# Turned tokens kept dense by feature block instead of interleaved, in an attention block on one core

## The chip, the cores and the metric

One core of a Trainium2 chip runs the whole program. The metric is the device time of one execution in microseconds (us); the time before is the median of three runs.

## The reference

The block gets 4 sequences of 1024 tokens with 512 features, f32. Cut to what matters:

```python
xn = layernorm(x)                                            # (4, 1024, 512)
q  = rope(rmsnorm(xn @ Wq + bq, qn_w))                       # 16 heads of 128
lk = rope(rmsnorm(xn @ Wlk + blk, kn_w)); lv = xn @ Wlv + blv
w  = softmax((xn @ Wcmp + bcmp).reshape(C, 4))               # C = 256 groups of 4 tokens
entries = einsum('cr,crh->ch', w, xn.reshape(C, 4, 512))     # weighted sum of each group
ck = rope(rmsnorm(entries @ Wk + bk, kn_w)); cv = entries @ Wv + bv
# per token and head: softmax over the 8 best of its causal ck scores, and a
# softmax over the band of this and the 128 tokens before
merged = (sparse @ cv + local @ lv) * 0.5
out = x + merged @ Wo + bo + fp8_rounded(xn) @ fp8_rounded(input2)
```

## The kernel before

**Chunks and units.** The 4096 tokens are cut into 32 chunks of 128 (t = 0 to 31, c = t mod 8 is the place within a sequence). For each chunk the heads go in eight units of two heads (u = 0 to 7). One loop runs over all 256 units s = 8t + u, and each of its passes works on several units at once, in an order written out by hand: TensorE does the scores of unit s (`scores`, L718 to L728), the queries and keys of s + 3 (`queries`, L576), the output product of s - 2 (`to_output`, L921), the values of s + 1 (`values_of`, L682) and the contexts of s - 1 (`values`, L888). VectorE masks the scores and finds the eight best (`weigh`, L750 to L773), settles the sparse weights, normalizes and rotates queries and keys, and turns 32 x 32 blocks.

**What goes through DRAM.** A full 128 x 128 turn is done in two halves: VectorE transposes 32 x 32 blocks within their partitions, and a write to DRAM followed by a read in another order moves the blocks to the right partitions. This is done for the probabilities (`turn`, L829 and L837, tile pr; `fetch`, L871, tile probT), for queries and keys (`turn_keys`, L657 and L660, tile thb, and L665, tile qk; `fetch_keys`, L675) and for the normalized tokens. All these transfers are issued by SyncE (SP), in program order. In a pass its queue holds, in this order: the write of the probabilities pr, whatever chunk preparation issues, the four key writes, the four fetches of probT, the two key fetches, and, in u = 2, the four fetches of the tokens of the next chunk. A transfer that has to wait holds up those behind it.

**Chunk preparation.** `chunk_prep(t)` is a generator that advances by two steps in each pass (`steps`). It loads a chunk, normalizes it (tile x_norm), weighs it for the pooled entries (L372 to L384), and in its step A3, which falls into u = 2, transposes the blocks (L392, x_norm to xb) and writes xb to DRAM (L397). In u = 3 it multiplies by the group weights (L403) and sums groups of four tokens (L411, tile few), and writes few (L420). Four chunks ahead of use is the rule; in the first chunks two are prepared in one chunk. Chunk 0 is turned by TensorE instead (`turn_tokens_here`, L460 and L462), and its entries are made by `add_tokens_here` (L437, L443). `chunk_entries` fetches the pooled sums back (L501) and multiplies them by the key and value weights (L511).

**The turned tokens.** `fetch_tokens` (L471) brings the tokens of a chunk into xnT: feature in the partition, and in each partition the element of token s and feature block k at s * 4 + k. So a 128 x 128 block for TensorE, which loads it as the stationary operand, is read at a step of four f32:

```python
xnT[:, :, k] if k or not t else xone,      # queries, L578
xnT[:, :, k],                              # values_of, L684
```

`put_ones` (L478) copies block 0 into a dense tile xone, for the chunks after the first, and sets its first row to one, which brings in the bias. `chunk_eight` rounds xnT to the values of an eight-bit float and multiplies the result x8 (bf16) by input2 (L558).

Of the kernel before, what the change touches and what calls it, by code (L numbers as in the profile page):

```python
# [12 lines left out]
F32 = mybir.dt.float32  # L13
# [6 lines left out]
P = 128  # L20
D = 128
RATIO = 4
ROPE = 64
HALF = ROPE // 2
BLK = 32
NB = P // BLK
# [12 lines left out]
def kernel(  # L39
# [299 lines left out]
    def chunk_prep(t):  # L339

        xt = x_tiles.pop(("norm", t))
        st = work.tile([P, 8], F32, tag="lnst", name=f"lnst_{t}")
        nc.vector.bn_stats(st[:, 0:6], xt)
        nc.vector.bn_aggr(st[:, 6:8], st[:, 0:6])
        r = rstd_of(st[:, 7:8], 1, 1.0, EPS_LN, f"lnr_{t}")
        yield "A0"
        yield "B0"
        if t:

            off = work.tile([P, 2], F32, tag="off", name=f"off_{t}")  # L350
            nc.gpsimd.tensor_scalar(off[:, 0:1], st[:, 6:7], -1.0, None, ALU.mult)
            nc.scalar.activation(
                xt, xt, AF.Identity, bias=off[:, 0:1], scale=1.0, accum_out=off[:, 1:2]
            )
            nc.gpsimd.tensor_scalar(off[:, 1:2], off[:, 1:2], 1.0 / HID, None, ALU.mult)
            mean = off[:, 1:2]
        else:
            mean = st[:, 6:7]
        yield "A1"
        nc.vector.tensor_scalar(xt, xt, mean, r, ALU.subtract, ALU.mult)  # L360
        yield "B1"
        if not t:
            turn_tokens_here(xt)
            yield "T"

        xb = scratch(f"xb_{t}")
        log = work.tile([P, 1], F32, tag="log", name=f"log_{t}", bufs=1)
        row = work.tile([P, 2, BLK], F32, tag="row", name=f"row_{t}", bufs=1)  # L370
        red = work.tile([P, BLK // RATIO], F32, tag="red", name=f"red_{t}", bufs=1)
        nc.vector.scalar_tensor_tensor(  # L372
            xb, xt, 1.0, wcmp_sb, ALU.mult, ALU.mult, accum_out=log
        )
        nc.vector.tensor_scalar(row[:, 0, :], ones, log, bcmp_sb, ALU.mult, ALU.add)
        nc.vector.transpose(row[:, 1, :], row[:, 0, :])
        fours = row[:, 1, :].rearrange("p (n r) -> p n r", r=RATIO)

        def wide(v):
            return v.unsqueeze(2).to_broadcast([P, BLK // RATIO, RATIO])  # L380

        nc.vector.tensor_reduce(red, fours, AX.X, ALU.max)
        nc.vector.tensor_tensor(fours, fours, wide(red), ALU.subtract)
        nc.scalar.activation(row[:, 1, :], row[:, 1, :], AF.Exp)  # L384
        yield "A2"
        yield "B2"
        if not t:
            yield from add_tokens_here(row, red, xb, wide)
            return


        nc.vector.transpose(  # L392
            xb.rearrange("p (b j k) -> p b k j", b=NB, k=KK),
            xt.rearrange("p (k b i) -> p b k i", b=NB, k=KK),
        )
        tokens[t] = dram.tile([P, HID], F32, tag="xb", name=f"xb_dram_{t}", bufs=GC + 2)
        nc.sync.dma_start(tokens[t], xb)  # L397
        yield "A3"
        nc.vector.tensor_reduce(red, fours, AX.X, ALU.add)
        nc.vector.reciprocal(red, red)  # L400
        nc.vector.tensor_tensor(fours, fours, wide(red), ALU.mult)
        yield "B3"
        nc.vector.tensor_tensor(  # L403
            xt.rearrange("p (b j k) -> p b j k", b=NB, k=KK),
            xb.rearrange("p (b j k) -> p b j k", b=NB, k=KK),
            row[:, 1:2, :].unsqueeze(3).to_broadcast([P, NB, BLK, KK]),
            ALU.mult,
        )
        yield "A4"
        few = work.tile([P, P], F32, tag="few", name=f"few_{t}", bufs=1)  # L410
        nc.vector.tensor_reduce(  # L411
            few.rearrange("p (n k) -> p n k", k=KK),
            xt.rearrange("p (n r k) -> p n k r", r=RATIO, k=KK),
            AX.X,
            ALU.add,
        )
        g, i = divmod(t, GC)
        if g not in pooled:
            pooled[g] = dram.tile([GC, P, P], F32, tag="pooled", name=f"pooled_{g}")
        nc.sync.dma_start(pooled[g][i], few)  # L420
        yield "B4"

    def add_tokens_here(row, red, xb, wide):

        few = scratch("few_here")
        nc.gpsimd.memset(few, 0.0)
        fours = row[:, 1, :].rearrange("p (n r) -> p n r", r=RATIO)
        nc.vector.tensor_reduce(red, fours, AX.X, ALU.add)
        nc.vector.reciprocal(red, red)
        nc.vector.tensor_tensor(fours, fours, wide(red), ALU.mult)  # L430
        nc.vector.transpose(row[:, 0, :], row[:, 1, :])
        wp = pp("weights_here")
        nc.tensor.matmul(
            wp[:, 0:P], row[:, 0, 0:1].to_broadcast([P, P]), ident, start=True, stop=True
        )
        yield "W"
        nc.vector.tensor_tensor(  # L437
            xb.rearrange("p (s k) -> p s k", k=KK),
            chunks[0][0],
            wp[:, 0:P].unsqueeze(2).to_broadcast([P, P, KK]),  # L440
            ALU.mult,
        )
        nc.vector.tensor_reduce(  # L443
            few[:, 0 : NE * KK].rearrange("p (n k) -> p n k", k=KK),
            xb.rearrange("p (n r k) -> p n k r", r=RATIO, k=KK),
            AX.X,
            ALU.add,
        )
        few_here.append(few)
        few_here.append(dram.tile([P, P], F32, tag="few_here", name="few_dram", bufs=1))  # L450
        nc.sync.dma_start(few_here[1], few[:, 0 : NE * KK])
        yield "B4"
# [3 lines left out]
    def turn_tokens_here(xt):  # L456

        xp = pp("xp")
        for k in range(KK):
            nc.tensor.transpose(xp[:, ts(k, P)], xt[:, ts(k, P)], ident)  # L460
        xnT = work.tile([P, P, KK], F32, tag="xnT", name="xnT_0")
        nc.scalar.copy(  # L462
            xnT.rearrange("p s k -> p k s"), xp.rearrange("p (k s) -> p k s", k=KK)
        )
        chunks[0] = (xnT, None)

    def fetch_tokens(t):
        xnT = work.tile([P, P, KK], F32, tag="xnT", name=f"xnT_{t}")
        turned = tokens.pop(t).rearrange("(a i) (b x) -> b i a x", a=NB, b=NB)
        for b in range(NB):  # L470
            nc.sync.dma_start(  # L471
                xnT[ds(b * BLK, BLK)].rearrange("i (a j) k -> i a (j k)", a=NB), turned[b]
            )
        chunks[t] = (xnT, work.tile([P, P], F32, tag="xone", name=f"xone_{t}"))

    def put_ones(t):
        xnT, xone = chunks[t]
        nc.scalar.copy(xone, xnT[:, :, 0])  # L478
        nc.gpsimd.memset(xone[0:1], 1.0)

    def chunk_entries(g, n):
# [64 lines left out]
    def chunk_eight(t):  # L546

        yield
        xt, xnT = x_tiles["sum", t], chunks[t][0]
        x8 = work.tile([P, KK * P], BF16, tag="x8", name=f"x8_{t}", bufs=1)  # L550
        src = xnT.rearrange("p s k -> p (s k)")
        yield from quantize(x8, src, scales[:, 0:1], f"x_{t}")
        nc.gpsimd.tensor_tensor(xt, xt, bo_sb, ALU.add)
        yield
        x8 = x8.rearrange("p (s k) -> p s k", k=KK)
        fp = pp(f"fp_{t}")
        for k in range(KK):
            nc.tensor.matmul(  # L558
                fp, x8[:, :, k], w2_sb[:, k, :], start=(k == 0), stop=(k == KK - 1)
            )  # L560
        yield
        nc.vector.scalar_tensor_tensor(xt, fp, inv, xt, ALU.mult, ALU.add)
# [8 lines left out]
    def queries(n):  # L571
        t, u = place(n)
        xnT, xone = chunks[t]
        qp = psum.tile([P, 512], F32, tag="qp", name=f"qp_{n}")
        for k in range(KK):
            nc.tensor.matmul(  # L576
                qp,
                xnT[:, :, k] if k or not t else xone,  # L578
                wqk_sb[u][:, k, :],
                start=(k == 0),  # L580
                stop=(t > 0 and k == KK - 1),
            )
        if not t:
            nc.tensor.matmul(  # L584
                qp, sel[:, u : u + 1].to_broadcast([P, P]), bias_b, start=False, stop=True
            )
        ss = work.tile([P, 4], F32, tag="ss", name=f"ss_{n}")
        units[n] = {"qp": qp, "ss": ss}
# [88 lines left out]
    def values_of(n):  # L677
# [3 lines left out]
        for k in range(KK):  # L681
            nc.tensor.matmul(  # L682
                vp[:, 0:256],
                xnT[:, :, k],  # L684
                wlv_sb[u][:, k, :],
                start=(k == 0),
                stop=(k == KK - 1),
            )
# [419 lines left out]
```

## Time and profile before

| | |
|---|---|
| median of three runs | 2717.2 us (2714.86 to 2717.34) |
| the profiled execution | 2725.88 us |
| its span, first to last instruction | 2723.7 us |
| granted TensorE clock | 0.992 |
| DMA engines, mean busy share | 56% on SyncE's queue |
| transfers of the tokens to DRAM, xb_dram | 31 of 256 KB, 2.2 us from issue to landing |
| fetches of the tokens, xnT | 124 of 64 KB, 2.3 us |

The busy shares of the engines are shares of the span. PE is the matmuls of TensorE and PEld its loads of the stationary operand, which run beside matmuls. Each f32 matmul shows as two records. The chain is followed back from the last instruction, at each step to what released it or to the instruction before it on its engine. In the groups, a line has the program line, the engine, the operation, the tile written and those read, the shape and the count; then busy us, mean ns of one; then the idle time of the engine just before them and who ended it. SPq is SyncE's queue of transfers; its length of a transfer is the time that the issue took.

### The profile page before, as it was taken

To read this page: it belongs to the slowest core of one execution; us is meant where nothing else is said; L and a number is where in the kernel's file an instruction comes from. 1 tells how busy PE (TensorE), PEld (TensorE's weight loads), DVE (VectorE), ACT (ScalarE), POOL (GpSimd) and SP (SyncE) were. 2 spreads that over 40 slices of the span, in tenths; PEclk is the share of its full clock that TensorE was granted. 3 is DMA by queue.
4 is the path that set the end of the run, shared out by engine and by line. 5 is a ranking of instruction groups with operands and counts; after the bars stand their busy time and mean duration, and the time that the engine had idled before them with its cause. 6 is when DMAs were issued, how large, how long until landed. Compare 5 with 4: busy or idle time off the path is not lost.

```text
span 2723.7 us, 46686 instructions
## 1 busy us (share of the span) xinstructions
PE 2652.3 (97%) x11802; PEld 2086.2 (77%) x11837; DVE 2318.3 (85%) x8884; ACT 1257.7 (46%) x5067; POOL 799.1 (29%) x1151
## 2 busy tenths in 40 slices
PE   8999999999999999999999999999999999999997
PEld 5777777777777777777777778777777777777776
DVE  7888888898888888888988888888988888888885
ACT  3444444444444444444444444444444444444443
POOL 4522332223332223232233322232323323222221
PEclk9999999999999999999999999999999999999998
DMA  8455455665545555566555555655665555566653
GB/s 257 120 142 150 132 149 167 171 165 153 154 135 158 151 157 149 161 166 169 160 145 139 155 151 154 170 159 157 168 164 146 150 141 147 151 161 165 162 153 107
DMA packets 667067, 422.85 MB, mean 155 GB/s; under 512 B 326528, under 2 KB 616112, under 8 KB 666800
## 3 DMA queue, kind: packets, MB, share of 16 engines
q1 hardware_dynamic: 666192, 419.46, 56.0%
q8 instruction: 97, 1.59, 0.3%
q14 instruction: 170, 1.39, 0.2%
q10 hardware_dynamic: 608, 0.41, 0.1%
HBM read 225.42 MB, written 194.25 MB: 154 GB/s over the span
## 4 chain that ended last, share of the span: by engine, by line
PE 76%; DVE 11%; DMA 5%; SPq 3%; ACT 3%; issue 2%; POOL 1%; DVEq 0%; ACTq 0%
PE qp L576 25%; PE vp L682 13%; PE cp L888 12%; PE op L921 12%; PE sc L728 5%; PE sc L725 4%; PE sc L718 3%; DMA probT<-pr 2%; SPq L665 1%; SPq L871 1%; ACT prob L775 1%; DVE probB L829 1%; DVE sc L750 1%; DVE taken L773 1%; PE fp L558 1%
## 5 line engine op out<-in xcount | busy, mean ns | idle before, releaser
L576 PE MATMUL qp<-wqk,xnT 128*128 128x512 f32 x1552 | 711.5, 595 | 3.5 <-DMA wqk<-in_L_attn_Wlk_dram 3.5
L576 PEld LDWEIGHTS qp<-wqk,xnT 128*128 128x128 f32 x1552 | 478.0, 309 | 221.4 <-issue 64.9
L775 ACT ACTIVATE prob<-sc,neg 128x256 f32<-128x256 f32 (+1 forms) x512 | 235.9, 461 | 879.2 <-DVE taken L773 861.1
L682 PEld LDWEIGHTS vp<-wlv,xnT 128*128 128x128 f32 x2048 | 517.8, 325 | 91.9 <-issue 56.2
L682 PE MATMUL vp<-wlv,xnT 128*128 128x256 f32 x2048 | 516.4, 395 | 0.1
L921 PE MATMUL op<-wo,cT 128*128 128x512 f32 x1024 | 481.6, 593 | 3.4 <-ACT cT L903 3.3
L325 POOL TENSOR_TENSOR rb<-th,cs 128x256 f32<-128x256 f32 x256 | 204.1, 797 | 949.7 <-DVE th L604 941.6
L750 DVE CUSTOM_DVE_ANT_0 sc<-sc,mask_b 128x256 f32<-128x256 f32 (+1 forms) x512 | 210.9, 412 | 180.8 <-PE sc L728 170.8
L811 ACT ACTIVATE prob<-prob,tot 128x256 f32<-128x256 f32 (+1 forms) x512 | 225.6, 488 | 300.3 <-DVE tot L801 297.6
L921 PEld LDWEIGHTS op<-wo,cT 128*128 128x128 f32 x1024 | 193.6, 190 | 206.8 <-issue 144.9
L888 PE MATMUL cp<-probT,lv 128*128 128x128 f32 x1920 | 307.0, 281 | 38.6 <-DMA probT<-pr 37.0
L888 PEld LDWEIGHTS cp<-probT,lv 128*128 128x128 f32 x1920 | 279.2, 197 | 55.8 <-issue 46.4
L311 ACT ACTIVATE junk<-qp 128x128 bf16<-128x128 f32 x1024 | 278.7, 272 | 30.6 <-PE qp L584 6.2
L604 DVE SCALAR_TENSOR_TENSOR th<-qp,r,norm_w 128x128 f32<-128x128 f32 x1024 | 286.2, 343 | 0.9 <-POOL r L306 0.9
L829 DVE STREAM_TRANSPOSE probB<-prob 128x512 f32<-128x512 f32 (+2 forms) x494 | 282.2, 609 | 0.1
L306 POOL TENSOR_TENSOR r<-r,nhalf 128x4 f32<-128x4 f32 x256 | 266.7, 1042 | 21.4
L305 POOL TENSOR_SCALAR r<-ss 128x4 f32<-128x4 f32 x256 | 61.6, 241 | 696.9 <-ACT junk L311 693.6
L791 DVE SCALAR_TENSOR_TENSOR prob<-taken,prob 128x128 f32<-128x128 bf16 (+7 forms) x512 | 182.8, 358 | 96.3 <-ACT prob L783 95.0
L888 PE MATMUL cp<-probT,cv 128*128 128x128 f32 x1536 | 259.9, 279 | 0.0
L576 PE MATMUL qp<-wqk,xone 128*128 128x512 f32 x496 | 258.5, 603 | 0.0
L728 PE MATMUL sc<-ckT,qT 128*128 128x96 f32 (+7 forms) x1024 | 228.2, 305 | 2.7 <-ACT ckT L543 2.7
L888 PEld LDWEIGHTS cp<-probT,cv 128*128 128x128 f32 x1536 | 217.3, 196 | 0.0
(143 smaller groups left out, 3844.9 us busy)
## 6 DMA issues: line engine op xcount, KB each, us to landing
pr<-probB SPq DMA_DIRECT2D x127, 512.0 KB, 3.3
probT<-pr SPq DMA_DIRECT2D x508, 128.0 KB, 3.0
qk<-thb SPq DMA_DIRECT2D x992, 64.0 KB, 1.8
pr<-probB SPq DMA_DIRECT2D x96, 384.0 KB, 2.3
probT<-pr SPq DMA_DIRECT2D x384, 96.0 KB, 2.5
qT<-qk SPq DMA_DIRECT2D x248, 128.0 KB, 2.9
lkT<-qk SPq DMA_DIRECT2D x248, 128.0 KB, 3.1
x_norm<-_attn_hidden_states_dram SPq DMA_DIRECT2D x32, 256.0 KB, 3.3
```

The costliest lines, as they stand in the source:

```text
L306: nc.gpsimd.tensor_tensor(r, r, nhalf[: ss.shape[0], 0:n], ALU.pow)
L311: nc.scalar.activation(junk[: src.shape[0]], src, AF.Square, accum_out=acc)
L576: nc.tensor.matmul(qp, xnT[:, :, k] if k or not t else xone, wqk_sb[u][:, k, :], start=(k == 0), stop=(t > 0 and k == KK - 1),)
L604: nc.vector.scalar_tensor_tensor(th[:, i, :], qp[:, ts(i, D)], r[:, i : i + 1], norm_w[:, i // 2, :], ALU.mult, ALU.mult,)
L682: nc.tensor.matmul(vp[:, 0:256], xnT[:, :, k], wlv_sb[u][:, k, :], start=(k == 0), stop=(k == KK - 1),)
L728: nc.tensor.matmul(sc[:, spa], q, ckT[:, 0:m], start=True, stop=True)
L750: nc.vector.tensor_tensor_reduce(sc[:, h, loc], sc[:, h, loc], mask_b[:, loc], -1.0, TAKEN, ALU.add, ALU.min, neg[h][0],)
L775: nc.scalar.activation(probs[h][:, loc], sc[:, h, loc], AF.Exp, bias=neg[h][0], scale=-1.0, accum_out=tot[:, h, 0:1],)
L811: nc.scalar.mul(probs[h][:, loc], probs[h][:, loc], tot[:, h, 0:1])
L829: nc.vector.transpose(pb[:, :, ds(h * g, g), :], prob[:, parts[0] * P : (parts[-1] + 1) * P].rearrange("p (g b i) -> p b g i", b=NB, i=BLK),)
L888: nc.tensor.matmul(blocks(cp[:, h, :]), v, probT[:, :, h * len(parts) + i - parts[0], :], start=(i == parts[0]), stop=(i == parts[-1]),)
L921: nc.tensor.matmul(op, cT[:, h, :], wo_sb[u][:, h, :], start=(u == 0 and h == 0), stop=(u == NU - 1 and h == 1),)
```

## The change

The turned tokens get another order: in each partition token s of feature block k stands at k * 128 + s, so that each block is dense. The block transposes write xb as (block b, k, token j of 32); the write to DRAM is cut into four transfers, one for each group of 32 partitions, of 512 runs of 32 elements (128 bytes), and does the permutation; in DRAM each feature has its 512 elements of k, a, j in one run of 2 KB, which the four fetches read. The readers of xnT, xb and x8 follow: the product and the sum of chunk preparation, the weight loads of queries, values and x8, and the first chunk's copy. The tile few keeps its order.

```diff
--- before.py
+++ after.py
@@ -390,27 +390,31 @@
 
 
         nc.vector.transpose(
-            xb.rearrange("p (b j k) -> p b k j", b=NB, k=KK),
+            xb.rearrange("p (b k j) -> p b k j", b=NB, k=KK),
             xt.rearrange("p (k b i) -> p b k i", b=NB, k=KK),
         )
-        tokens[t] = dram.tile([P, HID], F32, tag="xb", name=f"xb_dram_{t}", bufs=GC + 2)
-        nc.sync.dma_start(tokens[t], xb)
+        tokens[t] = dram.tile([BLK, NB * KK, NB, BLK], F32, tag="xb", name=f"xb_dram_{t}", bufs=GC + 2)
+        for a in range(NB):
+            nc.sync.dma_start(
+                tokens[t].rearrange("i f a j -> a i f j")[a],
+                xb[ds(a * BLK, BLK)].rearrange("i (f j) -> i f j", j=BLK),
+            )
         yield "A3"
         nc.vector.tensor_reduce(red, fours, AX.X, ALU.add)
         nc.vector.reciprocal(red, red)
         nc.vector.tensor_tensor(fours, fours, wide(red), ALU.mult)
         yield "B3"
         nc.vector.tensor_tensor(
-            xt.rearrange("p (b j k) -> p b j k", b=NB, k=KK),
-            xb.rearrange("p (b j k) -> p b j k", b=NB, k=KK),
-            row[:, 1:2, :].unsqueeze(3).to_broadcast([P, NB, BLK, KK]),
+            xt.rearrange("p (f j) -> p f j", j=BLK),
+            xb.rearrange("p (f j) -> p f j", j=BLK),
+            row[:, 1:2, :].to_broadcast([P, NB * KK, BLK]),
             ALU.mult,
         )
         yield "A4"
         few = work.tile([P, P], F32, tag="few", name=f"few_{t}", bufs=1)
         nc.vector.tensor_reduce(
-            few.rearrange("p (n k) -> p n k", k=KK),
-            xt.rearrange("p (n r k) -> p n k r", r=RATIO, k=KK),
+            few.rearrange("p (b e k) -> p b k e", b=NB, k=KK),
+            xt.rearrange("p (b k e r) -> p b k e r", b=NB, k=KK, r=RATIO),
             AX.X,
             ALU.add,
         )
@@ -435,14 +439,14 @@
         )
         yield "W"
         nc.vector.tensor_tensor(
-            xb.rearrange("p (s k) -> p s k", k=KK),
+            xb.rearrange("p (k s) -> p k s", k=KK),
             chunks[0][0],
-            wp[:, 0:P].unsqueeze(2).to_broadcast([P, P, KK]),
+            wp[:, 0:P].unsqueeze(1).to_broadcast([P, KK, P]),
             ALU.mult,
         )
         nc.vector.tensor_reduce(
-            few[:, 0 : NE * KK].rearrange("p (n k) -> p n k", k=KK),
-            xb.rearrange("p (n r k) -> p n k r", r=RATIO, k=KK),
+            few[:, 0 : NE * KK].rearrange("p (n k) -> p k n", k=KK),
+            xb.rearrange("p (k n r) -> p k n r", r=RATIO, k=KK),
             AX.X,
             ALU.add,
         )
@@ -458,24 +462,22 @@
         xp = pp("xp")
         for k in range(KK):
             nc.tensor.transpose(xp[:, ts(k, P)], xt[:, ts(k, P)], ident)
-        xnT = work.tile([P, P, KK], F32, tag="xnT", name="xnT_0")
-        nc.scalar.copy(
-            xnT.rearrange("p s k -> p k s"), xp.rearrange("p (k s) -> p k s", k=KK)
-        )
+        xnT = work.tile([P, KK, P], F32, tag="xnT", name="xnT_0")
+        nc.scalar.copy(xnT.rearrange("p k s -> p (k s)"), xp)
         chunks[0] = (xnT, None)
 
     def fetch_tokens(t):
-        xnT = work.tile([P, P, KK], F32, tag="xnT", name=f"xnT_{t}")
-        turned = tokens.pop(t).rearrange("(a i) (b x) -> b i a x", a=NB, b=NB)
+        xnT = work.tile([P, KK, P], F32, tag="xnT", name=f"xnT_{t}")
+        turned = tokens.pop(t).rearrange("i (b k) a j -> b i (k a j)", b=NB)
         for b in range(NB):
             nc.sync.dma_start(
-                xnT[ds(b * BLK, BLK)].rearrange("i (a j) k -> i a (j k)", a=NB), turned[b]
+                xnT[ds(b * BLK, BLK)].rearrange("i k s -> i (k s)"), turned[b]
             )
         chunks[t] = (xnT, work.tile([P, P], F32, tag="xone", name=f"xone_{t}"))
 
     def put_ones(t):
         xnT, xone = chunks[t]
-        nc.scalar.copy(xone, xnT[:, :, 0])
+        nc.scalar.copy(xone, xnT[:, 0, :])
         nc.gpsimd.memset(xone[0:1], 1.0)
 
     def chunk_entries(g, n):
@@ -548,15 +550,15 @@
         yield
         xt, xnT = x_tiles["sum", t], chunks[t][0]
         x8 = work.tile([P, KK * P], BF16, tag="x8", name=f"x8_{t}", bufs=1)
-        src = xnT.rearrange("p s k -> p (s k)")
+        src = xnT.rearrange("p k s -> p (k s)")
         yield from quantize(x8, src, scales[:, 0:1], f"x_{t}")
         nc.gpsimd.tensor_tensor(xt, xt, bo_sb, ALU.add)
         yield
-        x8 = x8.rearrange("p (s k) -> p s k", k=KK)
+        x8 = x8.rearrange("p (k s) -> p k s", k=KK)
         fp = pp(f"fp_{t}")
         for k in range(KK):
             nc.tensor.matmul(
-                fp, x8[:, :, k], w2_sb[:, k, :], start=(k == 0), stop=(k == KK - 1)
+                fp, x8[:, k, :], w2_sb[:, k, :], start=(k == 0), stop=(k == KK - 1)
             )
         yield
         nc.vector.scalar_tensor_tensor(xt, fp, inv, xt, ALU.mult, ALU.add)
@@ -575,7 +577,7 @@
         for k in range(KK):
             nc.tensor.matmul(
                 qp,
-                xnT[:, :, k] if k or not t else xone,
+                xnT[:, k, :] if k or not t else xone,
                 wqk_sb[u][:, k, :],
                 start=(k == 0),
                 stop=(t > 0 and k == KK - 1),
@@ -681,7 +683,7 @@
         for k in range(KK):
             nc.tensor.matmul(
                 vp[:, 0:256],
-                xnT[:, :, k],
+                xnT[:, k, :],
                 wlv_sb[u][:, k, :],
                 start=(k == 0),
                 stop=(k == KK - 1),
```

## The prediction

> **What bounds the kernel now.** I read the shares of busy time first, then the chain of work that ended last, then the groups of the engine they point to, then SyncE's queue at the place of the edit. The first two, from the page:
>
> ```profile
> PE 2652.3 (97%) x11802; PEld 2086.2 (77%) x11837; DVE 2318.3 (85%) x8884; ACT 1257.7 (46%) x5067; POOL 799.1 (29%) x1151
> ...
> PE 76%; DVE 11%; DMA 5%; SPq 3%; ACT 3%; issue 2%; POOL 1%; DVEq 0%; ACTq 0%
> ```
>
> TensorE is nearly never idle and three quarters of the chain run over it. The chain inside one steady pass of the unit loop (chunk 11) shows what such a pass is made of:
>
> ```profile
> 1000.08 3.44 PE qp L576 x8
> 1003.51 1.72 PE op L921 x4
> 1005.23 1.85 PE vp L682 x8
> 1007.09 1.34 PE cp L888 x12
> ```
>
> Columns: start, length, what. The piece is pure TensorE: 8 array runs for queries and keys (4 feature blocks, two runs each), 4 for the output, 8 for the values, then contexts and scores. From one start to the next this is 3.44/8 = 430 ns and 1.72/4 = 430 ns at 512 columns, 1.34/12 = 112 ns at 128 columns, and 1.85/8 = 231 ns at the 256 columns of the values. A straight line through 112 and 430 gives 112 + 318 x 128/384 = 218 ns at 256 columns. The values are 13 ns above it. The groups by shape say why:
>
> ```profile
> L682 PEld LDWEIGHTS vp<-wlv,xnT 128*128 128x128 f32 x2048 | 517.8, 325 | 91.9 <-issue 56.2 <-DVE prob L791 2.4 <-DVE th L604 1.7
> L576 PEld LDWEIGHTS qp<-wqk,xnT 128*128 128x128 f32 x1552 | 478.0, 309 | 221.4 <-issue 64.9 <-DMA pr<-probB 1.2 <-DMA cse<-in_rope_dram 0.2
> ...
> L576 PEld LDWEIGHTS qp<-wqk,xone 128*128 128x128 f32 x496 | 82.2, 191 | 1.3
> ```
>
> After the first bar stand busy us and the mean ns of one load. A block of turned tokens read at a step of 16 bytes (xnT) takes 309 to 325 ns to load, the same block copied to a dense tile (xone) 191. Behind a 512-column matmul of 430 ns the long load is covered; behind a 256-column one of 218 it isn't quite.
>
> **The change, part by part.** (1) Weight loads become dense: all xnT loads should take 191 ns. The queries gain nothing, since they already start every 430 ns; the 96 to 128 bf16 matmuls of L558 (512 columns, loads of 113 ns) neither. The values gain 2048 x (231 - 218) = 27.7 us, **-28**. Bounds: the scores at 256 columns, whose weights step by 8 bytes, take 0.44 for two in the chain, 220 ns, so at least 2048 x 11 = 22 us; half of a 512-column start is 215, so at most 33.
>
> (2) What a shorter pass loses. The waits list has "PE cp L888 <- DMA probT<-pr: 37.0, 26": in 26 of the passes the contexts wait for turned probabilities, whose path (scores, VectorE, a write to DRAM, a fetch) starts at the scores of the pass before. Such a wait gives back what up to two passes have gained, 2 x 8 x 13 ns = 0.21 us. 26 x 0.21 = 5.5, **+6**; bounds 0 and three places in each of 28 chunks, 18.
>
> (3) VectorE's shorter forms:
>
> ```profile
> L829 DVE STREAM_TRANSPOSE probB<-prob 128x512 f32<-128x512 f32 x254 | 164.9, 688 | 0.0
> ...
> L392 DVE STREAM_TRANSPOSE xb<-x_norm 128x512 f32<-128x512 f32 x31 | 33.6, 1084 | 0.0
> L411 DVE TENSOR_REDUCE few<-x_norm 128x128 f32<-128x512 f32 x31 | 33.0, 1063 | 1.1
> ...
> L403 DVE TENSOR_TENSOR x_norm<-xb,row 128x512 f32<-128x512 f32 x31 | 20.3, 656 | 0.1
> ```
>
> The transpose that wrote at a step of 16 bytes now writes runs as L829 does: 1084 - 688 = 0.40 us less. The reduction that read at such a step now reads dense, as L403 (656 ns): 0.41 less; its 128 results still go out at a step. The product of L403 stays. Both shortened operations stand on VectorE ahead of the key transposes (thb) that SyncE waits for, in the passes u=2 and u=3. The page has VectorE idle for 15%, which hides most of this; where the chain goes through thb (the chunks of the start, with two preparations each) it counts. I take 0.4 us in 12 of the 31 preparations (the seven up to chunk 3, and five later), **-5**; bounds 0 and 31 x 0.81 = 25. In the first chunk L462's strided copy on ScalarE (1067 ns; the dense copies of 128x256 take 369, so some 700) and L443 (1067 against 656) save about 0.8 once, **-1**. ScalarE's copies into xone (425 ns, 31) are off the chain: nothing.
>
> (4) The fetch of the tokens keeps its four transfers, but each partition's 2 KB is one run instead of four of 512 B. In the trace's packet records 2048 B take 84 ns and 512 B 27 to 42, so per chunk 128 x 84/16 engines = 0.7 us of transfer instead of 512 x 35/16 = 1.1. It is not waited for by TensorE (its users come a pass and more later); ScalarE's xone waits for it, 33.8 us in all, off the chain. Nothing; if the cover is gone, 0.4 us a chunk in our favour.
>
> (5) The write of the tokens: one transfer of 128 runs of 2 KB becomes four of 512 runs of 128 B. SyncE's queue around one such write (chunk 12, u=2), and the nearest relative of the new form, the fetch of pooled tokens, which is four transfers of 512 runs of 128 B in the other direction:
>
> ```profile
> 1080.40 0.34 SPq L837 DMA_DIRECT2D pr<-probB  x1
> 1081.41 0.34 SPq L397 DMA_DIRECT2D xb_dram<-xb  x1
> 1083.11 1.78 SPq L665 DMA_DIRECT2D qk<-thb  x4
> 1085.00 1.83 SPq L871 DMA_DIRECT2D probT<-pr  x4
> ...
> 1362.43 0.34 SPq L837 DMA_DIRECT2D pr<-probB  x1
> 1362.87 3.06 SPq L501 DMA_DIRECT2D fewT<-pooled  x4
> ```
>
> **Issue.** Between the write (done at 1081.75) and the key writes (1083.11, when VectorE's thb is ready) SyncE has 1.36 us free. Four issues at L501's median of 488 ns and 0.05 between take 2.1 instead of 0.34. With the transpose 0.40 earlier they run from 1081.0 to 1083.1, and thb is ready at 1082.7: the key writes start when they did before. At the 3.06 of the row above, 0.9 later. Queued behind on SyncE are the key writes, the four fetches probT that the contexts wait for, the key fetches, the token fetch and x_sum.
>
> **Transfer.** Key writes move their first bytes 0.8 us after issue, so the tokens move from 1081.8. 2048 packets over 16 engines, at 13 ns each (the 128-byte reads in the packet records), take 1.7 us and are paced by the issue; all is gone by 1084, before the key writes' first bytes. At 36 ns, the upper quartile of 512-byte packets, the key writes' among them, they last until 1081.8 + 4.6 = 1086.4. Behind them come the key writes, 512 x 33/16 = 1.05, and the fetches, 512 x 58/16 = 1.85: 1089.3 instead of 1086.83 + 0.8 + 0.46 = 1088.1. The margin is read here:
>
> ```profile
> 1088.44 2.02 PE L682 MATMUL vp<-wlv,xnT 128*128 128x256 f32 x8
> 1090.29 0.61 PE L888 MATMUL cp<-probT,lv 128*128 128x128 f32 x4
> ```
>
> The last fetch is issued at 1086.4 and lands 2.7 to 3.0 later, at 1089.1 to 1089.4; the contexts start at 1090.29, a margin of some 0.9, of which part 2 takes 0.2. So the late issue alone costs 0 to 0.2 per write, 36 ns a packet 1.2 - 0.7 = 0.5. Times 31: 0 to 6 at 13 ns, 15 at 36 ns; nothing here can gain, since no wait is removed. I take 0.2 x 31 = **+6**, by the fetch of the same shape. The key fetches behind have a further pass before use.
>
> A rule speaks against this part: the Trainium skill, "DMA: Bandwidth & Descriptors", Specifications, has transfers at line rate from 512 B on and says that below this the engine reads, modifies and writes. No write of 128 B is in this trace; the 128-byte reads took 13 ns and show nothing of it. If the rule doubles a short write to 70 ns, part 5 would be what the slow rival below has instead of 6.
>
> **Sum:** -28 + 6 - 5 - 1 + 6 = -22. The profiled execution took 2725.88 around its span of 2723.7; the median of the runs is 2717.2, 0.3% lower, and the steps are taken off it unscaled: **2695**.
>
> **Rivals.** *Short writes block the queue (slower).* Place: the 16 rings in u=2, between the tokens and the fetch of probT. At 70 ns a packet, twice a 512-byte packet's 35, the tokens last until 1081.8 + 9.0 = 1090.8 and the fetches until 1093.7, 5.6 late; less 0.7, 4.9 per write, 152 us: 2717 - 28 + 152 = 2841 (parts 2 and 3 cancel). It decides from the packet time at which 31 stalls eat 28 us, 0.9 each: 1.6 late, 39 ns. For it: no 128-byte write is in the trace. Against: it must cost more than packets four times as long, and 4096 against 2048 B (159, 84 ns) and 128 against 256 (13, 18) show time falling with size.
> *The wait for probT swallows the gain.* For it: 26 waits already, and margins of under 1 us in u=1 to u=3. Then half of part 1 and all of part 3 are lost: -14 + 6 - 1 = -9, 2708. Against: the steady pieces of the chain hold no VectorE at all.
> *VectorE's relief comes through in full.* -28 + 6 - 25 - 1 = -48: 2669. For it: both operations stand ahead of thb in the passes where contexts wait. Against: VectorE is idle 170.8 us waiting for scores (L728) and passes no gain on there.
> *The load is not what spaces the values.* Then part 1 is nothing: -6 + 12 = +6, 2723. Against: the other strided loader of 256 columns, L511, also takes 1.85 for 8 in the chain.
>
> **Numbers.** About 0.2% (5.4 us) can be told from no change. Forecast 0.53 (own range 2684 to 2704: part 1 from 22 to 33, the write from 0 to 15), swallowed gain 0.14, full relief 0.12, no effect of the load 0.04, slow writes 0.17. Faster takes the first three less 0.02 of the second, 0.77; same has that 0.02, half of the fourth and 0.02 of the slow rival near 39 ns, 0.06; slower the other 0.02 and 0.15, 0.17. The range takes in the swallowed gain, the upper bounds of parts 2 and 5, and part of the relief: 2677 to 2716, leaving out the far relief and the slow writes.
>
> **What would show it.** Right: xnT loads near 191 ns, eight values in 1.73 to 1.76, L392 near 0.69 and L411 near 0.65, probT waits on TensorE not above 50 us. Wrong: 128-byte packets above 39 ns, key writes of more than 3 us issue after the tokens, or a wait of several us at the contexts after every u=2.

## The result, and the profile after

| | before | after |
|---|---|---|
| median of the runs, same chip | 2717.27 us (2714.32 to 2719.55, 8 runs) | 2723.3 us (2720.71 to 2725.61, 8 runs) |
| the profiled execution | 2725.88 us | 2722.31 us |
| its span | 2723.7 us | 2720.3 us |

The ratio of after to before is 1.0021, 95% interval 1.0012 to 1.0030: slower by 6 us, where 22 us less were forecast. The profiled execution of before lay 9 us above its median and that of after 1 us below, so the two spans differ the other way; where the size of a difference matters, the ratios decide, and the traces say where it arises.

Shares of busy time, the chain by engine and the groups of the values, the queries and the contexts, from the page of the changed kernel:

```profile
PE 2623.6 (96%) x11837; PEld 1786.8 (66%) x11837; DVE 2296.4 (84%) x8884; ACT 1249.1 (46%) x5067; POOL 799.8 (29%) x1151
...
PE 66%; DVE 14%; DMA 7%; SPq 5%; ACT 4%; issue 3%; POOL 1%; DVEq 0%; ACTq 0%; POOLq 0%
...
L578 PEld LDWEIGHTS qp<-wqk,xnT 128*128 128x128 f32 x1552 | 295.1, 191 | 373.0 <-issue 372.2
L684 PEld LDWEIGHTS vp<-wlv,xnT 128*128 128x128 f32 x2048 | 389.4, 190 | 161.1 <-issue 115.9
...
L684 PE MATMUL vp<-wlv,xnT 128*128 128x256 f32 x2048 | 483.8, 379 | 0.0
...
L890 PE MATMUL cp<-probT,lv 128*128 128x128 f32 x1920 | 308.4, 281 | 57.7 <-DMA probT<-pr 55.5
```

The dense loads are there: 190 ns instead of 325 and 309, and the weight loads of TensorE fall from 77% to 66% of the span. The values' matmuls start every 216 ns instead of 231. But the chain runs less over TensorE (76% to 66%) and more over VectorE (11% to 14%), transfers (5% to 7%) and SyncE's queue (3% to 5%), and the contexts wait 55.5 us for turned probabilities where it was 37.0.

The tile view of xb (minimum, median and maximum in ns, then first and last start) shows the two operations that the change made shorter and longer:

```profile
L398 SPq DMA_DIRECT2D xb_dram<-xb x124: 567/627/1793, 58.9 to 2319.4; - x124
L392 DVE STREAM_TRANSPOSE xb<-x_norm x31: 667/669/704, 58.2 to 2316.8; 128x512 f32<-128x512 f32 x31
```

The transpose takes 669 ns (it was 1084), the sum into few 687 (1063). The write of the tokens, once 0.34 us of SyncE's time, is now four issues of 627 ns each. SyncE's queue in u = 2 of chunk 12, from the timeline of after (start, length, what):

```profile
1085.20 0.34 SPq L839 DMA_DIRECT2D pr<-probB  x1
1085.80 2.62 SPq L398 DMA_DIRECT2D xb_dram<-xb  x4
1088.52 2.02 SPq L667 DMA_DIRECT2D qk<-thb  x4
1090.64 1.84 SPq L873 DMA_DIRECT2D probT<-pr  x4
1092.64 0.38 SPq L677 DMA_DIRECT2D qT<-qk  x1
```

The same part of TensorE's timeline:

```profile
1092.80 1.89 PE L684 MATMUL vp<-wlv,xnT 128*128 128x256 f32 x8
1095.22 0.68 PE L890 MATMUL cp<-probT,lv 128*128 128x128 f32 x4 [0.53 <-DMA probT<-pr]
```

There is no free stretch on SyncE any more: the key writes come 0.1 us after the last token write, the fetches of probT 0.1 us after the key writes. Before, the key writes were issued 2.71 us after pr; now it is 3.32. The fetches are all issued 7.28 us after pr instead of 6.43. And TensorE, which went from values to contexts without a gap, now stands 0.53 us.

This happens in most chunks. By the landing events of the trace, the mean over chunks 4 to 27 of the time at which TensorE is ready for the contexts of u = 2, less that at which probT has landed, was +0.84 us before and is -0.49 now. This margin was never the same in all chunks: before it ran from -0.1 to 3.0 us and was below zero in one of the 24, now it is below zero in 20. The pass u = 3, where these contexts run, shows it: counted from its first score matmul to that of u = 4, it takes 289.6 us together over chunks 4 to 30, from 272.3. Every other pass of these chunks became shorter, by 1.5 to 5.2 us. In the chunks 0 to 3, where some chunks prepare two others, u = 2 takes 4.7 us longer. (The expectations below count the stalls in another way, by gaps between matmuls, as 24.5 us in u = 3 here and 22.8 us in u = 6 of e4.)

### The profile page after: what moved, and what is told of

Same layout as the page of the kernel before. It is cut to its first block, busy times and chain, and to the rows that moved or that the text cites. A ratio compares the mean times of both kernels' runs of the same rounds, so it can differ in the third digit from the quotient of the medians.

```text
span 2720.3 us, 46866 instructions
## 1 busy us (share of the span) xinstructions
PE 2623.6 (96%) x11837; PEld 1786.8 (66%) x11837; DVE 2296.4 (84%) x8884; ACT 1249.1 (46%) x5067; POOL 799.8 (29%) x1151
## 4 chain that ended last, share of the span: by engine, by line
PE 66%; DVE 14%; DMA 7%; SPq 5%; ACT 4%; issue 3%; POOL 1%; DVEq 0%; ACTq 0%; POOLq 0%
PE qp L578 21%; PE cp L890 12%; PE op L923 10%; PE vp L684 10%; PE sc L730 4%; DMA probT<-pr 4%; PE sc L727 4%; PE sc L720 3%; SPq L873 3%; SPq L667 2%; DVE sc L752 2%; DVE probB L831 2%; ACT prob L777 2%; DVE taken L775 1%; DVE top L770 1%
## 5 line engine op out<-in xcount | busy, mean ns | idle before, releaser
L578 PEld LDWEIGHTS qp<-wqk,xnT 128*128 128x128 f32 x1552 | 295.1, 191 | 373.0 <-issue 372.2
L684 PEld LDWEIGHTS vp<-wlv,xnT 128*128 128x128 f32 x2048 | 389.4, 190 | 161.1 <-issue 115.9
L684 PE MATMUL vp<-wlv,xnT 128*128 128x256 f32 x2048 | 483.8, 379 | 0.0
L890 PE MATMUL cp<-probT,lv 128*128 128x128 f32 x1920 | 308.4, 281 | 57.7 <-DMA probT<-pr 55.5
```

What stands on the lines that cost most here:

```text
L578: nc.tensor.matmul(qp, xnT[:, k, :] if k or not t else xone, wqk_sb[u][:, k, :], start=(k == 0), stop=(t > 0 and k == KK - 1),)
L684: nc.tensor.matmul(vp[:, 0:256], xnT[:, k, :], wlv_sb[u][:, k, :], start=(k == 0), stop=(k == KK - 1),)
L890: nc.tensor.matmul(blocks(cp[:, h, :]), v, probT[:, :, h * len(parts) + i - parts[0], :], start=(i == parts[0]), stop=(i == parts[-1]),)
```

## The experiments

The theory to begin with was the length of the issue: four issues of short runs hold SyncE until after thb is ready, in front of a fetch with less than 1 us to spare. The rivals: the transfers themselves (short packets in the rings ahead of probT), the strain of writing instead of reading short runs, or a gain of the dense blocks that was never there. In all these runs the kernel before, on the same chip, lay at 2722 to 2723 us.

**e1: the permutation on the side of the read.** The blocks stay dense, VectorE's forms short. The write is one transfer of 512 runs of 512 B; the four fetches read the short runs.

```diff
+        tokens[t] = dram.tile([KK, P, P], F32, tag="xb", name=f"xb_dram_{t}", bufs=GC + 2)
+        nc.sync.dma_start(
+            tokens[t].rearrange("k p x -> p k x"), xb.rearrange("p (k x) -> p k x", k=KK)
+        )
...
+        turned = tokens.pop(t).rearrange("k (a i) (b j) -> b i (k a) j", a=NB, b=NB)
```

> Dense blocks as in the changed kernel, but the permutation is done by the fetch: one write of 512 runs of 512 B per chunk, four fetches of 512 runs of 128 B. Theory I (SyncE's time to issue four short-run writes, 2.6 to 2.9 us in place of 0.34, holds up the key writes and the fetch of probT in u=2): the write costs 0.4 us on SyncE again, so the stall of the contexts in u=3 goes back to that of before, about 22 us of it in chunks 4 to 30, and the value matmuls' 30 us remain: 2695 to 2703. Theory II (the 128-byte packets themselves crowd the DMA engines in u=2): as many of them, in the same pass, so 2715 to 2724. Theory III (a faster TensorE only waits longer for the probabilities, whatever the write): 2712 to 2720.

Measured: 2697.93 us, 0.9906 (0.9894 to 0.9919). So the dense blocks do bring their gain, and 31 us of it (1.0021 - 0.9906, of 2722) are lost by how the changed kernel writes. The 31 compares two ratios, each to its own runs of the kernel before, which lay at 2717 us there and at 2723 here; the two profiled executions are 24 us apart, so the loss is 24 to 31 us. The timeline of e1 at the same place:

```profile
1069.30 0.34 SPq L837 DMA_DIRECT2D pr<-probB  x1
1069.89 0.36 SPq L397 DMA_DIRECT2D xb_dram<-xb  x1
1071.63 1.79 SPq L665 DMA_DIRECT2D qk<-thb  x4
1073.53 1.80 SPq L871 DMA_DIRECT2D probT<-pr  x4
```

Between the write's issue and the key writes SyncE waits 1.38 us for thb. That is the room a longer issue has here.

**e2 and e3: the number of issues, and the shortness of the runs, one at a time.** e2 is e1 with its write cut in four of 128 runs of 512 B. e3 is the changed kernel with a single write of 2048 runs of 128 B (and, in return, short runs in the fetch):

```diff
+        tokens[t] = dram.tile([NB * KK, P, BLK], F32, tag="xb", name=f"xb_dram_{t}", bufs=GC + 2)
+        nc.sync.dma_start(
+            tokens[t].rearrange("f p j -> p f j"), xb.rearrange("p (f j) -> p f j", j=BLK)
+        )
```

> As the run before, but the write is cut into four transfers of 32 partitions (128 runs of 512 B each). Four issues near 0.43 us take 1.9 us of SyncE in u=2 in place of 0.4, against 2.6 to 2.9 in the changed kernel. Theory I: some two thirds of the loss comes back, 2705 to 2715. Theories II and III: no different from the run before by more than 3 us.

> Dense blocks, one write of 2048 runs of 128 B in place of four of 512, and four fetches of 512 runs of 128 B. It tells apart what the issue time goes with. If it goes with the number of transfers, the one write is issued in 0.4 to 0.7 us and by theory I the time is 2695 to 2705; if it goes with the number of runs, it takes about 2.5 us and the time is 2718 to 2726. Theory II: twice as many short packets as in the changed kernel, 2724 to 2735.

Measured: e2 2711.62 us, 0.9953 (0.9941 to 0.9965); e3 2709.02 us, 0.9942 (0.9929 to 0.9954). Each costs by itself: 13 us for four issues of long runs, 10 us for short runs in one issue. In e3 the issue is as short as in e1, by the tile view of xb:

```profile
L397 SPq DMA_DIRECT2D xb_dram<-xb x31: 359/360/2052, 61.9 to 2302.6; - x31
```

Its cost arises behind the write: the key writes, issued on time, take 1.99 us to issue by the median instead of 1.78 (they scatter, from 1.77 to 3.7), and the fetches end 0.30 later.

**e9: both together, in e3's layout.** e3 with its write cut in four.

> e3 with its one write of 2048 runs of 128 B cut into four of 512, each from 32 partitions, into the same DRAM order; the fetch is that of e1 to e3. With e1 (one write, 512 B runs), e2 (four, 512 B) and e3 (one, 128 B) this fills a square. If the number of transfers and the shortness of the runs cost on their own, the two losses against e1 add up (0.0047 + 0.0036): ratio 0.998 to 1.000. If only SyncE's time ahead of the key writes counts, and an issue of this form takes 0.45 us as in e2 and not 0.63 as in the changed kernel, whose runs lie at one common step, it stays with e2: 0.995 to 0.997.

Measured: 2718.33 us, 0.9985 (0.9976 to 0.9994), where 0.0047 and 0.0036 added to e1's ratio give 0.9989. The two add up. The second alternative had supposed issues of 0.45 us, and they took 0.51. The changed kernel, whose issues take 627 ns against e9's 514, lies 0.0036 above.

**e4 and e5: the same four writes, later.** In e4 they are issued at the end of the pass u = 4, in e5 at the end of u = 3.

```diff
+        unsent.append((t, xb))
...
+        if t < GC or u == 4:
+            send_tokens()
```

> The changed kernel, with its four short-run writes issued at the end of pass u=4 (in the first four chunks at the end of the pass that prepares them), behind the key fetches, in place of ahead of the key writes of u=2. Same transfers and packets. Theory I: SyncE is free there until the next probabilities are ready, so the stalls in u=3 fall to those of before: 2695 to 2705. Theory III: 2715 to 2724, since nothing is taken off the loop but the place of the writes.

> As the late writes of e4, whose stalls went from u=3 to u=6 (22.8 us in chunks 4 to 30, VectorE's qm_x of L278 waiting for the write out of the buffer that it takes over), but issued one pass earlier, at the end of u=3. If that buffer is what cost e4 its gain, the stalls in u=6 go back under 4 us and the ratio is 0.988 to 0.995. If SyncE or the loop has no room anywhere for 2.6 us of issue, the stalls show in u=4 and the ratio stays at 1.000 or above.

Measured: e4 2729.46 us, 1.0025 (1.0016 to 1.0034); e5 2721.33 us, 0.9992 (0.9983 to 1.0001). The stalls in u = 3 do go away (in e4 these passes take 270.4 us, in e1 268.8), and new ones come. In e4 VectorE's qm_x waits until the write has read its scratch buffer, as the tile view of xb_dram says among those who waited:

```profile
  DVE qm_x L278: 26.0, 18
```

and the passes u = 6 of chunks 4 to 30 take 20 us more than in e1. In e5 the passes u = 5 take 12 us more; there the write of the probabilities pr of u = 4, which stands behind the four issues, goes out 1.0 us later after its scores than in e1. So neither place takes the four writes for nothing: e5 for want of time on SyncE, e4 for the buffer.

**e6: the short writes added to the kernel before.** Its own write stays, and four short writes of xb go to a tile in DRAM that nothing reads.

> The kernel before, its own write of the tokens left in, and the four short-run writes added behind it into a DRAM tile that nothing reads. The cost of the new form alone, with weight loads and VectorE as before. Theory I: 2.6 to 2.9 us of SyncE ahead of the key writes in u=2, 0.9 to 1.3 us of stall at the contexts of u=3 in each of 31 chunks: ratio 1.010 to 1.016. Theory III (a faster TensorE finds its gain lost whatever the write does): under 1.004.

Measured: 2774.61 us, 1.0191 (1.0177 to 1.0205), 52 us or 1.7 per chunk, more than theory I had given it, with no dense block in the kernel: the writes alone are the cost. The fetches of probT are issued 1.73 us later than in the kernel before.

**e7: the four short writes issued by ScalarE.**

> The changed kernel, its four short-run writes issued by ScalarE at the same place in program order in place of SyncE. The same packets move in u=2, but SyncE's queue is free. Theory I: stalls in u=3 fall from 24.5 us (chunks 4 to 30) to below 8, and the ratio is 0.990 to 0.998, unless ScalarE is held up by issuing. If the packets and not the issue are the cost (theory II), u=3 keeps 20 us or more and the ratio is 1.000 or above.

Measured: 2721.51 us, 0.9995 (0.9986 to 1.0004). With the same packets in flight, issued from the same moment on (0.6 us after pr), probT of u = 2 lands 16.87 us after its scores, near the kernel before (16.79) and e1 (16.7), instead of 17.81. Against e1 the key writes start on time, but their issue takes 2.12 us instead of 1.78. But no time is won, because ScalarE is now held, by the tile view of xb_dram:

```profile
L398 ACTq DMA_DIRECT2D xb_dram<-xb x124: 556/639/1802, 59.6 to 2316.8; - x124
...
  ACT junk L311: 86.7, 18
```

Its sums of squares (junk) wait 86.7 us behind the issues. The passes u = 3 of chunks 4 to 30 take 10 us more than in e1, where the changed kernel's take 21 more, and the passes u = 4 now take 12 more. Neither theory's range fits: of the 1.1 us by which the changed kernel's probT lands later than e1's (table below), 0.3 stay when SyncE doesn't issue the writes.

**e8: how much VectorE's shorter forms are worth.** e1 with two reductions of 0.38 and 0.41 us, into a tile that nothing reads, in the places where the transpose and the sum have become shorter.

> The read-side permutation of e1, with one reduction over 256 elements (about 0.4 us) added on VectorE behind the block transpose and one behind the sum of four, so that VectorE's chunk preparation is as long as before. What it loses against e1 is what VectorE's shorter forms bring: 5 us by the prediction (ratio 0.9906 + 0.002), up to 25 us if both stand on the chain in every chunk (0.999).

Measured: 2704.65 us, 0.9930 (0.9918 to 0.9942): 6.5 us more than e1. In the profiled executions, 6.1 us apart, 3.9 us of it lie in chunks 0 to 3 and 4.4 in the passes u = 4 of chunks 4 to 27; other passes give some back. The passes u = 3 of these chunks lose 0.1, although the fetches of probT are issued 0.3 us later.

**e10, e11 and e12: issues with next to no transfer behind them.** To part the issue from the data, e1 was given four more transfers per chunk, behind its write, of which nothing is read: in e10 four writes of 32 runs of 4 B, in e11 four reads of 32 runs of 256 B, in e12 those reads issued by GpSimd. In e11 the addition reads:

```diff
+        for a in range(NB):
+            nc.sync.dma_start(spare[ds(a * BLK, BLK)], rope[ts(a, BLK), :])
```

> e1 with four more writes behind the write of the tokens, of 32 runs of 4 bytes each, into a DRAM tile that nothing reads: issue time without bytes. Theory I: four issues near 0.43 us take 1.9 us of SyncE, as e2's four, and the ratio is 0.994 to 0.998. Theory II: with next to no bytes nothing is lost, 0.990 to 0.992.

> e1 with four small reads added on SyncE behind the write of the tokens: 32 runs of 256 B each, 32 KB in all, from an input into a tile that nothing uses. It asks again what e10 could not tell, since 4-byte writes turned out to hold the rings for some 8 us: four issues with hardly any bytes, and no writes to DRAM. Theory I: four issues near 0.44 us are 1.9 us of SyncE as in e2, the probabilities of u=2 land some 0.4 to 0.6 us later after their scores than in e1 (16.7), and the ratio is 0.993 to 0.998. Theory II: 32 KB are nothing beside the 512 KB of probabilities, and the ratio is 0.990 to 0.992.

> The kernel of e11 (the layout of e1, and four reads of 32 runs of 256 B per chunk into a tile that nothing reads), with the four reads issued by GpSimd, at the same place of the program, in place of SyncE. Theory I, the time on SyncE's queue is what costs: e11 lost 28 us to e1 because its key writes were issued 3.22 us after the write of pr instead of 2.34 and its probT landed 9.67 instead of 8.80 us after it; with the reads on another queue the key writes are back at 2.3 to 2.4, probT lands at 8.8 to 9.0, and the ratio is that of e1, 0.9906, up to 0.993 if GpSimd is held up a little by issuing. Theory II, the transfers themselves, small packets in the rings just ahead of the key writes and of probT, are what costs: the same 128 packets fly at the same place, and the ratio stays near e11's 1.0008, 0.998 to 1.002, with probT landing 9.5 or later although the key writes are issued on time.

e10 was a miss as a probe: 2979.15 us, 1.0946 (1.0931 to 1.0961). Its timeline:

```profile
1108.51 0.36 SPq L397 DMA_DIRECT2D xb_dram<-xb  x1
1108.92 1.98 SPq L402 DMA_DIRECT2D spare<-ones  x4
1111.00 1.82 SPq L668 DMA_DIRECT2D qk<-thb  x4
1117.53 4.34 SPq L874 DMA_DIRECT2D probT<-pr  x4
```

The issues take what was expected, 1.98 us, but the first of the tiny writes lands only at 1117.5, 8.5 us after its issue, and the first fetch, which has the same completion semaphore, waits for that (in the waits of SyncE's queue: "SPq L874 <- DMA spare<-ones: 105.9, 50"). The key writes behind them land late too. This tells of 4-byte writes and says nothing of the issue.

e11 measured 2725.43 us, 1.0008 (0.9999 to 1.0016): 28 us more than e1, and more than either theory had given it. The timeline shows why:

```profile
1082.92 0.34 SPq L840 DMA_DIRECT2D pr<-probB  x1
1083.51 0.36 SPq L398 DMA_DIRECT2D xb_dram<-xb  x1
1083.91 2.12 SPq L402 DMA_DIRECT2D spare<-in_rope_dram  x4
1086.13 1.82 SPq L668 DMA_DIRECT2D qk<-thb  x4
1088.05 1.84 SPq L874 DMA_DIRECT2D probT<-pr  x4
```

The four reads come on top of the write's 0.36, so the key writes start 3.21 us after pr, nearly as late as in the changed kernel (3.32), though 32 KB are read and nothing short is written. The expectation had counted four issues as in e2 and had left out that e2's four replace the one. e12 takes only the issuing engine away; its tile view of spare:

```profile
L402 POOL DMA_DIRECT2D spare<-in_rope_dram x124: 496/496/745, 58.4 to 2289.6; - x124
```

It measured 2699.16 us, 0.9922 (0.9908 to 0.9935). With the same reads at the same place of the program, all but 4 of the 28 us are gone, and probT is issued and lands as in e1. But the reads don't fly at the same time, as the expectation had it. GpSimd runs ahead of SyncE:

```profile
1064.76 2.08 POOL L402 DMA_DIRECT2D spare<-in_rope_dram  x4
...
1067.55 0.34 SPq L840 DMA_DIRECT2D pr<-probB  x1
```

By the medians of chunks 4 to 27 it issues them from 2.6 us before pr on, SyncE in e11 from 1.0 us after. So e12 alone can't part the time on SyncE's queue from the transfers; the table below does.

**The runs side by side.** Medians over 27 chunks of what SyncE does in u = 2, in us after the issue of pr, read from the trace; the cost is against e1 (for e6 against before), from the ratios; the last two columns say how much longer two parts of the profiled execution are than in e1 (for e6 than in before): the passes u = 3 of chunks 4 to 27, and chunks 0 to 3. e4, e5 and e10 have their losses elsewhere, as told above.

| kernel | key writes start | fetches issued | probT landed | cost, us | u = 3 | chunks 0 to 3 |
|---|---|---|---|---|---|---|
| e1, one write, 512-B runs | 2.34 | 6.08 | 8.80 | 0 | 0 | 0 |
| e12, + four reads by GpSimd | 2.33 | 6.05 | 8.82 | 4 | -0.1 | 1 |
| e8, + 0.38 and 0.41 us on VectorE | 2.66 | 6.37 | 9.12 | 6.5 | 0.1 | 4 |
| e3, one write, 128-B runs | 2.33 | 6.38 | 8.94 | 10 | 5.5 | 5 |
| e2, four writes, 512-B runs | 2.72 | 6.50 | 9.37 | 13 | 7.0 | 5 |
| e9, four writes, 128-B runs | 2.95 | 6.79 | 9.69 | 22 | 11.8 | 10 |
| e7, the changed kernel's writes by ScalarE | 2.33 | 6.45 | 9.14 | 24 | 9.8 | 6 |
| e11, + four reads by SyncE | 3.22 | 7.10 | 9.67 | 28 | 12.6 | 11 |
| the changed kernel | 3.33 | 7.34 | 9.90 | 31 | 20.9 | 11 |
| before | 2.70 | 6.42 | 9.18 | 0 | 0 | 0 |
| e6, before + four short writes | 4.12 | 8.15 | 10.73 | 52 | 35.2 | 15 |

The kernels differ in run length, count, direction and layout; but for e7, where ScalarE is held, the cost rises with the delay of the fetches, as far as the ratios tell, which are good to some 3 us each. The transfers themselves are not slower: from the last fetch's issue to probT's landing it takes 2.6 to 2.9 us in every row, 2.56 in the changed kernel and 2.72 in e1. They are issued later. Of the changed kernel's delay of 1.26 us against e1, 0.99 is the later start of the key writes and 0.24 the first of them, which takes 0.56 us right behind the last token write instead of 0.32; 0.03 is the rest. In e7, with SyncE's queue free of the token writes, the key writes still take 0.34 us more; whether the short writes in flight do this, or ScalarE's issuing beside them, is not shown. No run issues the four short writes from GpSimd.

## Why the prediction was wrong

- **Bound and part 1 right.** TensorE is the bound, and the load spaced the values: 231 to 216 ns, times 2048 is 31 us, forecast 28, bounds 22 to 33. The rival in which the load has no effect falls. e1, the change without its costly write, measured -25.6 us, where parts 1 to 4 without part 5 had forecast -28.
- **Part 2, the shorter pass at the waits for probT (+6).** e8 has the dense loads without VectorE's relief and with one write: 0.9930 is -19, and -19 + 31 leaves 12 for this part, by difference and with what e1's own transfers cost in it. Twice the value, inside its bounds of 0 to 18. The wait doesn't swallow the gain.
- **Part 3, VectorE's shorter forms (-5).** 6.5 by e8, more than half of it in the first four chunks, as forecast. The two durations came out at 669 and 687 ns, forecast 688 and 656. The full relief falls.
- **Part 4, the fetch at nothing.** Not seen to cost; e1's fetches of short runs stand in the fastest kernel.
- **Part 5 is the step that failed.** It said: "Four issues at L501's median of 488 ns and 0.05 between take 2.1 instead of 0.34 ... the key writes start when they did before", and "So the late issue alone costs 0 to 0.2 per write". The runs show 2.62 us, key writes 0.63 us later than before and 0.99 later than the same kernel could have them, 0.24 more in the key writes' own issue, and a pass u = 3 that is 0.7 us longer per chunk than before and 0.9 longer than in e1. Against e1 that is 31 us by the ratios (24 by the traces), where 6 were taken and 15 were the upper bound. Three things were off.
  - The duration was borrowed from reads; the timeline of one such read, 3.06 us for four, stood in the prediction and was nearer than the median. For that row the prediction had the key writes 0.9 late, and the fetches did go out 0.92 later than before; what it made of this, 0.2, was far too little.
  - The margin, read from one pass (0.9, mean 0.84), was taken as if every chunk had it. It lay between -0.1 and 3.0, so a delay of its own mean size already stalls many chunks. That a delay inside the margin is free was right: e8's 0.3 us cost nothing in u = 3. The chunks 0 to 3, with their double preparations, lost 11 us against e1, and part 5 gave them no price of their own.
  - The shorter transpose was spent twice: part 3 counted it as time won in 12 preparations, part 5 used it in all to cover the late issue. By e8 that can explain 6.5 us at most.
- **The slow rival** had the place, u = 2 between the tokens and the fetch of probT, and the wrong mechanism. It needed packets of over 39 ns. In the packet records the writes of 128 B took 11 to 13 ns each, and a token write landed 2.2 us after its issue, by the median. The rule weighed there, of the Trainium skill, "DMA: Bandwidth & Descriptors", Specifications, that an engine reads, modifies and writes below 512 B, left no mark in these times at 128 B.
- **The signs of being wrong.** None of the three came: packets of 11 to 13 ns instead of over 39, key writes of 2.02 us issue instead of over 3, a mean wait of under 1 us and not of several at the contexts after u = 2. They fitted the slow rival alone. Of the signs of being right only the waits for probT failed, 55.5 us against 50.

The sum by the measured terms is -31 + 12 - 6.5 + 31 = +5.5, near the measured 6; part 2 was taken by difference, so this shows the sizes and is no second proof. The same page of the Trainium skill, "DMA: Bandwidth & Descriptors", bears on the cause in another place. Its section "Issuing engines are not separate DMA queues" says that issuing from several engines saves only the sequencer's time, usually small beside the transfer. e11 and e12 agree with what is saved, and show that it isn't small in its effect here: 2.1 us of issue on one queue or another are 1.0008 or 0.9922, though e12's reads also fly earlier.

The version that beats both kernels is e1: dense blocks, one issue in u = 2, and the short runs in the fetches, which stand behind probT in the queue and are used a pass and more later.

## What to carry to other kernels

A transfer costs the queue that issues it a time of its own, and what stands behind it on that queue pays: price an edit of a transfer by issues times the measured length of an issue in that form, at the place in the queue, against what the next time-critical fetch has to spare there. If a permutation needs more or shorter pieces, put them on the side of the transfer that has slack behind it, here the read instead of the write. Read that room over all chunks and not from one: here its mean was 0.84 us, and single chunks had nothing. Time that one part of a change wins can't cover another part's delay and be counted as a gain too.

## What the runs showed of the hardware that was not expected

- The issue of a write on SyncE depends on its form, not on its bytes or its number of runs alone: one transfer of 512 runs of 512 B and one of 2048 runs of 128 B both take 0.36 us; a quarter of the first takes 0.45 by the median, a quarter of the second 0.51 in e9's layout in DRAM and 0.63 in the changed kernel's. What sets this stays open.
- It also depends on what was issued just before. Of four key writes the first takes 0.32 us and each further one 0.43 to 0.45; in e2 and e9 too the first of the four token writes takes 0.32 and the others more. Right behind the last token write of the changed kernel the first key write takes 0.56, right behind the one of e1's form the first small read of e11 0.58. So four transfers cost more than four times a single issue, and part of a transfer's price can stand in the row of the next.
- 128-byte writes were quick, and 4-byte writes were not: in e10, 128 writes of 4 B to neighbouring addresses in each chunk put the landing of the key writes at 10.2 us after their issue instead of 1.76, and cost 281 us in the whole run.
